# Expert outputs added to the result in device memory by indirect accumulating transfers, in place of a gather and an add per token

## The chip, the cores and the metric

One Trainium2 chip, one core. A time is the device time of one execution in microseconds (us). TensorE (PE) multiplies matrices, VectorE (DVE) and ScalarE (ACT) work on rows, GpSimd (POOL) does the same more slowly and issues the indirect transfers, SyncE (SP) issues most of the plain transfers. Each engine runs its own instructions in order; a transfer is carried out by 16 DMA engines once an engine has issued it.

## The reference, cut to what matters

Everything is fp32. `x` holds 32 x 64 = 2048 tokens of 512 features.

```python
x = x + xattn0(layernorm(x), ctx)          # 32 query heads, 8 key heads, head size 128
x = x + ffn0(layernorm(x))                 # shared MLP 512 -> 1024 -> 512 and a latent path
x = x + xattn1(layernorm(x), ctx)          # 32 heads of size 16
x = x + ffn1(layernorm(x))                 # the part that is changed

def ffn1(h, W_gate, b_gate, W_e, b_e):     # 8 experts, 512 -> 512
    logits = h @ W_gate + b_gate
    _, top_idx = top_k(logits, 2)                             # two experts for each token
    y_all = relu(einsum('bsd,edh->bseh', h, W_e) + b_e)
    return take_along_axis(y_all, top_idx[..., None], 2).mean(axis=2)
```

## The kernel before, in words

The tokens lie in SBUF as 16 tiles `xs[0..15]` of 128 tokens x 512 features, in four chunks of 512 tokens. The kernel goes through the four layers one after the other.

**First attention (0 to about 1240 us).** A loop of 32 steps, each some 38 us long: one group of query heads for one chunk. Two steps that follow each other (a "visit") share a set of weights. `load_attn0` brings the set of the next visit to one of two halves of `weights`. POOL then forms sums of weight quarters: `left_sums` (L396 to L399) of the query weights and `right_sums` (L406 to L409) of the output weights. SP has little else to do in this stage, so that a transfer that waits for nothing is issued long before the step in whose code it stands.

**Lists of the experts.** For the last layer each expert has a list in device memory, `xg`. There are two groups of tokens: chunks 0 to 2 (group 0) and chunk 3 (group 1), and `xg[i]` has room for every token of the group in each of the 8 lists. The lists are set to zero by `clear_lists` (L283), 16 large transfers issued early by SP. Later `route_step` normalizes the rows of a chunk (`norm_row`), multiplies by the gate and finds each token's two experts and its place in their lists (`route_keep`, `route_places`). `route_row` (L1092) then scatters 128 rows at a time to the lists with an indirect transfer from POOL, two for each tile. This runs in the loop of the second attention, in which POOL also computes masks (L926) and the normalized head outputs (`attn1_mix`, L994 to L998). A scatter waits for the clearing transfers of its group.

**Blocks.** A list is worked off in blocks of 128 rows. How many blocks an expert needs is known only at run time, so the program has as many as can be needed: 31 for group 0 and 15 for group 1. `close_lists` computes for each block which expert it belongs to and at which row it starts (`bi`). `load_rows` (L1187, SP) loads four blocks at a time into a tile `xr` after all scatters of the group have landed. `block_turn` transposes a block (4 PE matmuls `px`, an ACT copy to `xT`), and `block_expert` multiplies it by the expert's weights (8 matmuls `py` at L105), adds the bias (DVE, L1217), applies the ReLU with factor 0.5 (ACT, L1218) and stores the 128 rows of `y` to `yg` (ACT, L1219). The tile `y` comes from a pool of seven buffers that `xT` shares, `xr` from a pool of four.

**The end.** When group 0's blocks are done, `gather` (L1223, POOL) fetches the two rows of `yg` that belong to each token of a tile by the places that `token_rows` worked out, and `combine` (L1232, L1233, DVE) adds them to `x` and stores the tile to `out` (L1234, SP). Group 0's tiles are gathered while PE works on group 1's blocks; group 1's four tiles follow after the last block.

Of the kernel before, what the change touches and what calls it, by code (L numbers as in the profile page):

```python
# [9 lines left out]
F32 = mybir.dt.float32  # L10
# [6 lines left out]
P = 128  # L17
# [6 lines left out]
NG = 8  # L24
NE = 8
EPS = 1e-5


@with_exitstack
def layers(ctx: ExitStack, tc: tile.TileContext, a: dict, out: bass.AP):  # L30
# [36 lines left out]

    mix_slots = [cells[:, 10240 + 512 * i : 10752 + 512 * i] for i in range(4)]
    route_rows, route_T = arena[:, 7], arena[:, 6]

    def t8(name):
        return work.tile([P, 4, 512], F32, tag="t8", name=name, bufs=4)

# [189 lines left out]


    GROUPS = [range(0, NC - 1), range(NC - 1, NC)]
    CAP = [len(cs) * CH for cs in GROUPS]
    NB = [2 * cap // P + NE - 1 for cap in CAP]
    xg = [dram.tile([NE * cap, HID], F32, name=f"xg{i}") for i, cap in enumerate(CAP)]
    yg = [dram.tile([nb * P, HID], F32, name=f"yg{i}") for i, nb in enumerate(NB)]

    start_row = const.tile([P, 2, NE], F32, tag="start_row", name="start_row")
    for i, cap in enumerate(CAP):
# [3 lines left out]
        )  # L276
    zero = const.tile([P, P], F32, tag="zero", name="zero")
    nc.gpsimd.memset(zero, 0.0)
# [349 lines left out]
    for i in range(len(order) + 1):  # L628
# [397 lines left out]

    counts, slots = {}, {}

# [32 lines left out]
    def route_places(c, keep):  # L1061
# [19 lines left out]
        pin(nc.vector.tensor_tensor(pos, tot[:, 0], run[:, 0:TT, :], ALU.add))  # L1081
        slots[c] = (pos, keep)
        return chosen(pos, keep, start_row[:, i, :], n)
# [34 lines left out]
    def close_lists(i):  # L1118
# [33 lines left out]
        )  # L1152
        pin(nc.vector.tensor_reduce(blk[:, 0, :], own, AX.X, ALU.add))
        pin(nc.vector.tensor_scalar(blk[:, 0, :], blk[:, 0, :], float(NE - 1), None, ALU.min))
        pin(
# [3 lines left out]
        )  # L1159
        pin(nc.vector.tensor_reduce(blk[:, 1, :], own, AX.X, ALU.add))  # L1160
        pin(nc.vector.tensor_tensor(blk[:, 1, :], steps[0:1, 0:nb], blk[:, 1, :], ALU.subtract))
        pin(
            nc.vector.tensor_scalar(
                blk[:, 1, :], blk[:, 1, :], float(top - 1), float(P), ALU.min, ALU.mult
            )
# [4 lines left out]
        pin(nc.vector.tensor_copy(bi, blk[:, 0:2, :]))  # L1170
        return bi, lst

    def token_rows(i, lst):
        n = f"l{i}"
        off = small.tile([P, NE], F32, tag="off", name=f"off_{n}", bufs=1)
        pin(nc.vector.tensor_scalar(off, lst[:, 1, :], float(P), None, ALU.mult))
        return [chosen(*slots[c], off, f"{n}_{c}") for c in GROUPS[i]]

    def load_rows(i, j0, bi):
        xr = t8(f"xr_{i}_{j0}")  # L1180
        for j in range(j0, min(j0 + 4, NB[i])):
            v = nc.values_load(
                bi[0:1, 1, j : j + 1], engines=[mybir.EngineType.SP],
                min_val=0, max_val=NE * CAP[i] - P,
                skip_runtime_bounds_check_because="an expert's list and a block within it",
            )
# [14 lines left out]

    def block_expert(i, j, xT, bi):
        n = f"{i}_{j}"
# [13 lines left out]
        pin(nc.vector.tensor_tensor(y, py, be1[:, bass.ds(v[1], 1), :], ALU.add))  # L1217
        nc.scalar.activation(y, y, AF.Relu, scale=0.5)  # L1218
        nc.scalar.dma_start(yg[i][j * P : (j + 1) * P, :], y)  # L1219

    def gather(i, u, t, at, ys):
        for r in range(2):
            nc.gpsimd.indirect_dma_start(  # L1223
                out=ys[:, r, :],
                out_offset=None,
                in_=yg[i],
                in_offset=bass.IndirectOffsetOnAxis(ap=at[u][:, r, t : t + 1], axis=0),
            )

    def combine(c, t, ys):  # L1230
        x = xs[c * TT + t]
        pin(nc.vector.tensor_tensor(ys[:, 0, :], ys[:, 0, :], ys[:, 1, :], ALU.add))  # L1232
        pin(nc.vector.tensor_tensor(x, x, ys[:, 0, :], ALU.add))  # L1233
        nc.sync.dma_start(out[(c * TT + t) * P : (c * TT + t + 1) * P, :], x)  # L1234

# [18 lines left out]
    def route_step(c, step):  # L1254
        n = f"e{c}"
        if step in ("rows0", "rows2"):
            t0 = int(step[-1])
            if t0 == 0:
                prep["h"] = route_rows if c < NC - 2 else t8(f"h_{n}")
            stats = row_stats([xs[c * TT + t0 + i] for i in range(2)], f"{n}_{t0}")  # L1260
            for i in range(2):
                norm_row(c, t0 + i, stats, prep["h"][:, t0 + i, :], i)
        elif step in ("turn0", "turn2"):
# [53 lines left out]
    for i in range(NI + 1):  # L1317
# [45 lines left out]
        if c == NC - 1 and b == 6:  # L1363
            lists.append([*close_lists(0)])
        for _ in range(2):
            if sends:
                route_row(*sends.pop(0))
        if c == NC - 1 and b == 1:
            load_experts(range(5, NE))

    blocks = [(0, j) for j in range(NB[0])] + [(1, j) for j in range(NB[1])]
    assert not sends
    first, xr, turned, done, waiting = NB[0], {}, None, 0, []
    between = {
# [3 lines left out]
    for m in range(len(blocks) + 1):  # L1380
        xT = turned
        if m < len(blocks):
            i, j = blocks[m]
            if j % 4 == 0:
                xr[i] = load_rows(i, j, lists[i][0])
            turned = block_turn(i, j, xr[i])
            if m == 0:
                attn1_out(NC * TT - 1, oTs.pop(NC * TT - 1), (0, 1))
        if m > 0:
            il, jl = blocks[m - 1]  # L1390
            block_expert(il, jl, xT, lists[il][0])
        for step in between.get(m, ()):
            route_step(NC - 1, step)
        if sends:
            route_row(*sends.pop(0))
        if m == 13:
            lists.append([*close_lists(1)])
# [69 lines left out]
```

## Time and profile before

| | |
|---|---|
| runs | 2019.36, 2020.13, 2022.64 us; median 2020.13 us |
| profiled execution | 2020.86 us, of which 2019.2 us are its span |
| PE busy | 1939.5 us (96% of the span) |
| DVE, ACT, POOL busy | 50%, 24%, 23% |
| granted clock of TensorE, mean | 0.988 |
| bytes moved by DMA | 155.39 MB |
| time of the first block's `py` / end of the last block's | about 1815 us / 1996.3 us |

A page of the profile gives the busy time of each engine, the chain of work that ended last, and the groups of instructions with the mean duration of one. A transfer's time "to landing" runs from the start of its issue to the semaphore update that says it has landed. Times on the page are microseconds unless they are marked ns.

### The profile page before, as it was taken

To read this page: it belongs to the slowest core of one execution; us is meant where nothing else is said; L and a number is where in the kernel's file an instruction comes from. 1 tells how busy PE (TensorE), PEld (TensorE's weight loads), DVE (VectorE), ACT (ScalarE), POOL (GpSimd) and SP (SyncE) were. 2 spreads that over 40 slices of the span, in tenths; PEclk is the share of its full clock that TensorE was granted. 3 is DMA by queue.
4 is the path that set the end of the run, shared out by engine and by line. 5 is a ranking of instruction groups with operands and counts; after the bars stand their busy time and mean duration, and the time that the engine had idled before them with its cause. 6 is when DMAs were issued, how large, how long until landed. Compare 5 with 4: busy or idle time off the path is not lost.

```text
span 2019.2 us, 26458 instructions
## 1 busy us (share of the span) xinstructions
PE 1939.5 (96%) x10576; PEld 1537.1 (76%) x10576; DVE 1011.8 (50%) x1961; ACT 494.5 (24%) x935; POOL 474.4 (23%) x502
## 2 busy tenths in 40 slices
PE   6999999999999999999999999999999999869995
PEld 5888888888888888888888887778787767545442
DVE  8445445445456445345345355365546676652324
ACT  1211211211212211111111112221113656433221
POOL 5010010010032110110111120144136545541024
PEclk9999999999999999999999999999999999889998
DMA  9993110110120110110110013000014002225457
GB/s 319 284 294 106 35 53 18 35 53 20 54 74 8 45 37 17 52 39 15 52 42 13 21 58 105 1 11 1 1 46 163 17 22 69 84 84 177 155 165 233
DMA packets 138233, 155.39 MB, mean 77 GB/s; under 512 B 5120, under 2 KB 88896, under 8 KB 138112
## 3 DMA queue, kind: packets, MB, share of 16 engines
q1 hardware_dynamic: 126096, 124.53, 19.8%
q0 software_dynamic: 5392, 17.11, 2.6%
q10 hardware_dynamic: 6624, 12.06, 1.6%
q8 instruction: 85, 1.39, 0.3%
q14 instruction: 36, 0.29, 0.0%
HBM read 94.44 MB, written 58.20 MB: 76 GB/s over the span
## 4 chain that ended last, share of the span: by engine, by line
PE 91%; DVE 5%; ACT 1%; DMA 1%; POOL 1%; issue 1%; POOLq 0%; SPq 0%; DVEq 0%; ACTq 0%
PE ppx_o L424 11%; PE pqx_a L424 8%; PE py L105 8%; PE sc_a L105 6%; PE pv_a L105 5%; PE ppz_o L424 5%; PE pqz_a L424 5%; PE pk_a L105 5%; PE po_o L105 3%; PE pp L105 3%; PE pdx_f L424 3%; PE ppy_o L424 3%; PE pqy_a L424 3%; PE pqv_a L424 3%; PE phx_f L424 2%; PE pq_b L105 2%
## 5 line engine op out<-in xcount | busy, mean ns | idle before, releaser
L105 PE MATMUL py<-arena,xT 128*128 x368 | 165.7, 593 | 0.0
L406 POOL TENSOR_TENSOR arena<-weights 128x512 f32<-128x512 f32 x16 | 20.7, 1295 | 563.2 <-PE ppz_o L424 563.2
L365 ACT ACTIVATE at_a<-at_a 128x512 f32<-128x512 f32 x64 | 40.4, 631 | 444.0 <-DVE at_a L364 444.0
L105 PEld LDWEIGHTS pv_a<-weights,arena 128*128 128x128 f32 x1024 | 119.4, 192 | 15.3 <-issue 15.3
L424 PE MATMUL ppx_o<-weights,oT_o 128*128 128x256 f32 x512 | 122.8, 383 | 0.1
L424 PE MATMUL pqz_a<-arena 128*128 128x256 f32 x512 | 121.0, 379 | 1.8 <-DVE qT_a L500 1.8
L105 PE MATMUL pk_a<-arena,weights 128*128 128x512 f32 x256 | 117.7, 603 | 3.6 <-issue 3.6
L424 PE MATMUL pqx_a<-arena,weights 128*128 128x256 f32 x512 | 121.0, 379 | 0.0
L105 PEld LDWEIGHTS sc_a<-kT_a,qT_a 128*128 128x128 f32 x1024 | 119.4, 192 | 1.7
L493 ACT ACTIVATE u_a<-pqx_a,bq 128x256 f32<-128x256 f32 x192 | 80.5, 470 | 163.2 <-PE pqx_a L424 163.2
L105 PE MATMUL pv_a<-weights,arena 128*128 128x128 f32 x1024 | 119.5, 275 | 0.0
L105 PE MATMUL sc_a<-kT_a,qT_a 128*128 128x64 f32 x1024 | 117.9, 273 | 0.0
L105 PEld LDWEIGHTS py<-arena,xT 128*128 128x128 f32 x368 | 66.3, 190 | 65.5 <-issue 65.5
L478 DVE COPY v_a<-pv_a 128x512 f32<-128x512 f32 x32 | 22.1, 690 | 179.8 <-PE pv_a L105 179.8
L584 DVE TENSOR_TENSOR x<-ppx_o,x 128x512 f32<-128x512 f32 x128 | 86.8, 678 | 45.7 <-PE ppx_o L424 43.9
L424 PEld LDWEIGHTS pqz_a<-arena 128*128 128x128 f32 x512 | 97.2, 190 | 15.3 <-issue 2.2
L424 PEld LDWEIGHTS ppx_o<-weights,oT_o 128*128 128x128 f32 x512 | 94.8, 190 | 12.0 <-ACT oT_o L574 0.5
L424 PEld LDWEIGHTS pqx_a<-arena,weights 128*128 128x128 f32 x512 | 94.8, 190 | 11.6
L500 DVE TENSOR_TENSOR qT_a<-pqz_a,u_a 128x512 f32<-128x512 f32 x64 | 44.2, 691 | 112.3 <-ACT u_a L493 80.3
L1217 DVE TENSOR_TENSOR y<-py,weights 128x512 f32<-128x512 f32 x46 | 31.8, 691 | 119.7 <-PE py L105 119.3
L105 PEld LDWEIGHTS pk_a<-arena,weights 128*128 128x128 f32 x256 | 49.3, 194 | 52.9 <-issue 51.5
L396 POOL TENSOR_TENSOR arena<-weights 128x512 f32<-128x512 f32 x18 | 23.2, 1290 | 243.5 <-PE pqz_a L424 240.5
(337 smaller groups left out, 3823.2 us busy)
## 6 DMA issues: line engine op xcount, KB each, us to landing
xg<-zero SPq DMA_DIRECT2D x8, 3072.0 KB, 18.0
weights<-in_Wq SPq DMA_DIRECT2D x16, 1024.0 KB, 5.3
weights<-in_Wo SPq DMA_DIRECT2D x16, 1024.0 KB, 5.2
xr<-xg SPq DMA_DIRECT2D x46, 256.0 KB, 3.4
yg<-y ACTq DMA_DIRECT2D x46, 256.0 KB, 3.0
weights<-in_Wkv SPq DMA_DIRECT2D x32, 256.0 KB, 2.8
arena<-in_ctxT SPq DMA_DIRECT2D x8, 1024.0 KB, 5.1
xg<-zero SPq DMA_DIRECT2D x8, 1024.0 KB, 13.0
```

Source lines behind the costliest of these rows:

```text
L105: nc.tensor.matmul(ps, lhsT, rhs, start=(i == 0), stop=(i == len(pairs) - 1))
L365: nc.scalar.activation(dst, dst, AF.Exp, scale=scale)
L396: engine.tensor_tensor(s1, a21, a22, ALU.add)
L406: engine.tensor_tensor(t1, b12, b11, ALU.subtract)
L424: nc.tensor.matmul(ps[:, m, :], left[:, k, m * P : (m + 1) * P], right[:, k, :], start=first and m == i == k == 0, stop=i == len(pairs) - ...
L478: nc.vector.tensor_copy(v, pv)
L493: nc.scalar.activation(u[:, m * 256 : (m + 1) * 256], ps[:, m * 256 : (m + 1) * 256], AF.Identity, bias=bq[:, 4 * g + 2 * heads + m : 4 * ...
L500: nc.vector.tensor_tensor(q5[:, heads, :, 4 * half : 4 * half + 4, :], ps.rearrange("p (m b q) -> p m b q", m=2, q=64), u.rearrange("p (m ...
L584: nc.vector.tensor_tensor(dst, ps.rearrange("p (m n) -> p m n", m=2), dst, ALU.add)
L1217: pin(nc.vector.tensor_tensor(y, py, be1[:, bass.ds(v[1], 1), :], ALU.add))
```

## The change

A row of a list is now `ROW` = 516 numbers: the 512 features, the token's number as an integer, the factor 0.5, and two numbers that fill it up. `route_step` writes the number and the factor beside the normalized rows with a POOL iota and a POOL memset for each two tiles. An empty row holds zeros, factor 0 and the number of a token of the other group; `clear_list` writes such rows to the lists from a tile `empty` with 130 transfers of 128 rows (97 for group 0, 33 for group 1), and between the groups POOL rewrites `empty`. A list has 128 more such rows at its end, to which the blocks that no expert needs now point.

The residual `x` of each tile is stored to `out` as soon as the second attention is done with it (`attn1_out`). A block's `y` is scaled by its rows' factors in the ReLU, and an indirect transfer from POOL adds its rows to the rows of `out` that the numbers name. `yg`, `token_rows`, `gather` and `combine` are gone. In the built program each such adding transfer waits for the one before it to have landed, for `y` (ACT) and for the load of its `xr`; the first one waits for the stores of `x` as well. Experts 4 to 7 are loaded late where before it was 5 to 7, because the slots beside them have moved by 16 numbers.

```diff
+ROW = HID + 4
-    mix_slots = [cells[:, 10240 + 512 * i : 10752 + 512 * i] for i in range(4)]
-    route_rows, route_T = arena[:, 7], arena[:, 6]
+    mix_slots = [cells[:, 10224 + 512 * i : 10736 + 512 * i] for i in range(4)]
+    route_T = cells[:, 12272:14320].rearrange("p (k n) -> p k n", k=KT)
+    route_rows = cells[:, 14320:16384].rearrange("p (t n) -> p t n", n=ROW)
...
-    xg = [dram.tile([NE * cap, HID], F32, name=f"xg{i}") for i, cap in enumerate(CAP)]
-    yg = [dram.tile([nb * P, HID], F32, name=f"yg{i}") for i, nb in enumerate(NB)]
+    xg = [dram.tile([NE * cap + P, ROW], F32, name=f"xg{i}") for i, cap in enumerate(CAP)]
...
+    def empty_rows(i):
+        nc.gpsimd.memset(empty, 0.0)
+        at = HID - 3 * QUARTER
+        nc.gpsimd.iota(
+            empty[:, at : at + 1].bitcast(I32), pattern=[[0, 1]], base=GROUPS[1 - i][0] * CH,
+            channel_multiplier=1,
+        )
...
-    def clear_lists(e):
-        for i, cap in enumerate(CAP):
+    def clear_list(i, e):
+        if e == 0:
+            empty_rows(i)
+        rows_of = xg[i][e * CAP[i] :, :]
+        for m in range(CAP[i] // P + (e == NE - 1)):
             ins = nc.sync.dma_start(
-                xg[i][e * cap : (e + 1) * cap, :].rearrange("(p m) (k n) -> p (m k) n", p=P, n=P),
-                zero[:, None, :].broadcast_to([P, cap // P * KT, P]),
+                rows_of[m * P : (m + 1) * P, :].rearrange("p (k n) -> p k n", n=QUARTER),
+                empty[:, None, :].broadcast_to([P, 4, QUARTER]),
             )
...
-            if i % 4 == 1:
-                clear_lists(i // 4)
+        if 8 <= i < 24:
+            clear_list(i // 16, i % 8)
...
+            if i == 1:
+                nc.sync.dma_start(out[k * P : (k + 1) * P, :], xs[k])
...
-        nc.scalar.activation(y, y, AF.Relu, scale=0.5)
-        nc.scalar.dma_start(yg[i][j * P : (j + 1) * P, :], y)
-
-    def gather(i, u, t, at, ys):
-        for r in range(2):
+        nc.scalar.activation(y, y, AF.Relu, scale=xr[:, j % 4, HID + 1 : HID + 2])
+        pin(
             nc.gpsimd.indirect_dma_start(
-                out=ys[:, r, :],
-                out_offset=None,
-                in_=yg[i],
-                in_offset=bass.IndirectOffsetOnAxis(ap=at[u][:, r, t : t + 1], axis=0),
-            )
-
-    def combine(c, t, ys):
-        x = xs[c * TT + t]
-        pin(nc.vector.tensor_tensor(ys[:, 0, :], ys[:, 0, :], ys[:, 1, :], ALU.add))
-        pin(nc.vector.tensor_tensor(x, x, ys[:, 0, :], ALU.add))
-        nc.sync.dma_start(out[(c * TT + t) * P : (c * TT + t + 1) * P, :], x)
+                out=out,
+                out_offset=bass.IndirectOffsetOnAxis(
+                    ap=xr[:, j % 4, HID : HID + 1].bitcast(I32), axis=0
+                ),
+                in_=y,
+                in_offset=None,
+                compute_op=ALU.add,
+            )
+        )
...
+            h = prep["h"][:, t0 : t0 + 2, :]
+            nc.gpsimd.iota(
+                h[:, :, HID : HID + 1].bitcast(I32), pattern=[[P, 2], [0, 1]],
+                base=(c * TT + t0) * P, channel_multiplier=1,
+            )
+            nc.gpsimd.memset(h[:, :, HID + 1 :], 0.5)
...
-    load_experts(range(5))
+    load_experts(range(4))
...
-        elif m == 15:
-            rows_of = [token_rows(i, lists[i][1]) for i in range(2)]
-        if m > first + 2 and done < len(GROUPS[0]) * TT:
-            u, t = divmod(done, TT)
-            ys = t4(f"ys_{u}_{t}")
-            gather(0, u, t, rows_of[0], ys)
-            waiting.append((GROUPS[0][u], t, ys))
-            done += 1
-        while waiting and (len(waiting) > 2 or m == len(blocks)):
-            combine(*waiting.pop(0))
-    ys = [t8(f"ys_{t}") for t in range(2)]
-    for t in range(TT):
-        gather(1, 0, t, rows_of[1], ys[t // 2][:, 2 * (t % 2) : 2 * (t % 2) + 2, :])
-    for t in range(TT):
-        combine(NC - 1, t, ys[t // 2][:, 2 * (t % 2) : 2 * (t % 2) + 2, :])
```

More of the change, by code (lines that the diff above doesn't have):

```diff
@@ L65, in layers, with list_rows @@
     ]
-    mix_slots = [cells[:, 10240 + 512 * i : 10752 + 512 * i] for i in range(4)]
-    route_rows, route_T = arena[:, 7], arena[:, 6]
+    mix_slots = [cells[:, 10224 + 512 * i : 10736 + 512 * i] for i in range(4)]
+    route_T = cells[:, 12272:14320].rearrange("p (k n) -> p k n", k=KT)
+    route_rows = cells[:, 14320:16384].rearrange("p (t n) -> p t n", n=ROW)
+    def list_rows(name):
+        return work.tile([P, 4, ROW], F32, tag="t8", name=name, bufs=4)
     def t8(name):
-        return work.tile([P, 4, 512], F32, tag="t8", name=name, bufs=4)
+        t = list_rows(name).rearrange("p i n -> p (i n)")
+        return t[:, 0:2048].rearrange("p (i n) -> p i n", i=4)
     def t4(name):
@@ L276, in layers @@
         )
-    zero = const.tile([P, P], F32, tag="zero", name="zero")
-    nc.gpsimd.memset(zero, 0.0)
+    QUARTER = ROW // 4
+    empty = const.tile([P, QUARTER], F32, tag="empty", name="empty")
+    def empty_rows(i):
[5 more added lines that the diff above has]
+        )
     clearings = ([], [])
     waits = mybir.DependencyInfo(mybir.DependencyClass.Sync, mybir.DependencyReason.DATA)
-    def clear_lists(e):
-        for i, cap in enumerate(CAP):
+    def clear_list(i, e):
[3 more added lines that the diff above has]
+        for m in range(CAP[i] // P + (e == NE - 1)):
             ins = nc.sync.dma_start(
-                xg[i][e * cap : (e + 1) * cap, :].rearrange("(p m) (k n) -> p (m k) n", p=P, n=P),
-                zero[:, None, :].broadcast_to([P, cap // P * KT, P]),
+                rows_of[m * P : (m + 1) * P, :].rearrange("p (k n) -> p k n", n=QUARTER),
+                empty[:, None, :].broadcast_to([P, 4, QUARTER]),
             )
@@ L1024, in attn1_queries @@
             )
-    counts, slots = {}, {}
+    counts = {}
     def route_parts(c, fT):
@@ L1081, in route_places @@
         pin(nc.vector.tensor_tensor(pos, tot[:, 0], run[:, 0:TT, :], ALU.add))
-        slots[c] = (pos, keep)
         return chosen(pos, keep, start_row[:, i, :], n)
@@ L1152, in close_lists @@
         )
-        pin(nc.vector.tensor_reduce(blk[:, 0, :], own, AX.X, ALU.add))
-        pin(nc.vector.tensor_scalar(blk[:, 0, :], blk[:, 0, :], float(NE - 1), None, ALU.min))
+        pin(nc.vector.tensor_reduce(blk[:, 0, :], own[:, :, 0 : NE - 1], AX.X, ALU.add))
         pin(
@@ L1159, in close_lists @@
         )
-        pin(nc.vector.tensor_reduce(blk[:, 1, :], own, AX.X, ALU.add))
+        pin(nc.vector.tensor_reduce(blk[:, 1, :], own[:, :, 0 : NE - 1], AX.X, ALU.add))
         pin(nc.vector.tensor_tensor(blk[:, 1, :], steps[0:1, 0:nb], blk[:, 1, :], ALU.subtract))
@@ L1163, in close_lists @@
             nc.vector.tensor_scalar(
-                blk[:, 1, :], blk[:, 1, :], float(top - 1), float(P), ALU.min, ALU.mult
+                blk[:, 1, :], blk[:, 1, :], float(top), float(P), ALU.min, ALU.mult
             )
@@ L1170, in close_lists @@
         pin(nc.vector.tensor_copy(bi, blk[:, 0:2, :]))
[L1171 to L1177, printed above, removed]
+        return bi
     def load_rows(i, j0, bi):
-        xr = t8(f"xr_{i}_{j0}")
+        xr = list_rows(f"xr_{i}_{j0}")
         for j in range(j0, min(j0 + 4, NB[i])):
@@ L1183, in load_rows @@
                 bi[0:1, 1, j : j + 1], engines=[mybir.EngineType.SP],
-                min_val=0, max_val=NE * CAP[i] - P,
+                min_val=0, max_val=NE * CAP[i],
                 skip_runtime_bounds_check_because="an expert's list and a block within it",
@@ L1200, in block_turn, with block_expert @@
         return xT
-    def block_expert(i, j, xT, bi):
+    def block_expert(i, j, xT, bi, xr):
         n = f"{i}_{j}"
@@ L1258, in route_step @@
             if t0 == 0:
-                prep["h"] = route_rows if c < NC - 2 else t8(f"h_{n}")
+                prep["h"] = route_rows if c < NC - 2 else list_rows(f"h_{n}")
+            h = prep["h"][:, t0 : t0 + 2, :]
[4 more added lines that the diff above has]
+            nc.gpsimd.memset(h[:, :, HID + 1 :], 0.5)
             stats = row_stats([xs[c * TT + t0 + i] for i in range(2)], f"{n}_{t0}")
             for i in range(2):
-                norm_row(c, t0 + i, stats, prep["h"][:, t0 + i, :], i)
+                norm_row(c, t0 + i, stats, prep["h"][:, t0 + i, 0:HID], i)
         elif step in ("turn0", "turn2"):
@@ L1363, in layers @@
         if c == NC - 1 and b == 6:
-            lists.append([*close_lists(0)])
+            lists.append(close_lists(0))
         for _ in range(2):
@@ L1368, in layers @@
         if c == NC - 1 and b == 1:
-            load_experts(range(5, NE))
+            load_experts(range(4, NE))
     blocks = [(0, j) for j in range(NB[0])] + [(1, j) for j in range(NB[1])]
     assert not sends
-    first, xr, turned, done, waiting = NB[0], {}, None, 0, []
+    xr, turned = {}, None
     between = {
@@ L1384, in layers @@
             if j % 4 == 0:
-                xr[i] = load_rows(i, j, lists[i][0])
-            turned = block_turn(i, j, xr[i])
+                xr[i, j // 4] = load_rows(i, j, lists[i])
+            turned = block_turn(i, j, xr[i, j // 4])
             if m == 0:
@@ L1390, in layers @@
             il, jl = blocks[m - 1]
-            block_expert(il, jl, xT, lists[il][0])
+            block_expert(il, jl, xT, lists[il], xr[il, jl // 4])
         for step in between.get(m, ()):
@@ L1396, in layers @@
         if m == 13:
[L1397 to L1412 removed]
+            lists.append(close_lists(1))
 def kernel(
```

## The prediction

> **What bounds the kernel now.** I read the page first, then the chain of work that ended last, then the end of the span by stretches and in order of time, then the rows of the transfers.
>
> ```profile
> span 2019.2 us, 26458 instructions
> PE 1939.5 (96%) x10576; PEld 1537.1 (76%) x10576; DVE 1011.8 (50%) x1961; ACT 494.5 (24%) x935; POOL 474.4 (23%) x502
> ```
>
> PE is busy nearly throughout, so time is to be had only where PE idles. The chain (start, length, what) ends so:
>
> ```profile
> 1981.63 3.44 PE py L105 x8
> 1985.50 3.43 PE py L105 x8
> 1989.37 6.88 PE py L105 x16
> 2009.75 4.86 DMA ys<-yg,at_l
> ```
>
> PE sets the pace to 1996.3, one block each 3.87 us (1985.50 to 1989.37). What follows is not PE's. The stretches (length, busy time of PE, PEld, DVE, ACT, POOL with counts, clock, DMA share, GB/s):
>
> ```profile
> 1900.00:1950.00 50.00, 50.00 (x155) 24.54 (x154) 8.95 (x13) 14.48 (x26) 5.43 (x6) 1.00 0.44 141
> 1996.50:2019.20 22.70, 0.00 (x0) 0.00 (x0) 8.59 (x13) 0.63 (x1) 8.03 (x8) 0.59 0.59 182
> ```
>
> For the last 22.7 us PE does nothing. The instructions there (start, length, engine, idle before it and releaser):
>
> ```profile
> 2000.55 0.95 POOL L1223 DMA_INDIRECT ys<-yg,at_l  x1 [7.03 <-DMA yg<-y]
> ...
> 2009.75 0.95 POOL L1223 DMA_INDIRECT ys<-yg,at_l  x1 [0.31 <-issue]
> ...
> 2014.70 0.69 DVE L1232 TENSOR_TENSOR ys<-ys 128x512 f32<-128x512 f32 x1 [0.50 <-DMA ys<-yg,at_l]
> 2015.43 0.69 DVE L1233 TENSOR_TENSOR x<-x,ys 128x512 f32<-128x512 f32 x1
> ```
>
> The last `y` is stored, eight gathers are issued one after the other, the last lands, two adds follow, and the store's landing ends the span. This is what the change can win. The rows of indirect transfers, issue and time to landing (min, median, max), first the scatters from 1724 to 1800 us, then the last eight gathers:
>
> ```profile
> L1092 POOL DMA_INDIRECT xg<-h_e,at_e x7: 979/1000/1007, 1774.8 to 1795.2; - x7
> ...
> DMA to landing us min/median/max: 2.7/2.8/4.4
> ```
> ```profile
> L1223 POOL DMA_INDIRECT ys<-yg,at_l x8: 947/953/1334, 2000.5 to 2009.8; - x8
> ...
> DMA to landing us min/median/max: 3.4/4.1/5.5
> ```
>
> **The change part by part.** All sums are made against the span of 2019.2 us. The profiled execution took 2020.86 us, 1.66 more than its span and 0.73 over the median of 2020.13; I carry the difference over to the median.
>
> *The end, if the adding transfers keep up.* PE's work is the same, so the last `py` still ends at 1996.3. DVE's bias (0.69) and ACT's ReLU (0.63) bring `y` at 1997.7; one adding transfer of time T then ends the span. With T = 3.8 that is 2001.5: 17.7 less. Gone with it are 32 gathers (0.95 each on POOL), 32 DVE adds (0.69 each) and 46 stores on ACT; PE's cover hides all but those of the last 22.7 us, so they count for nothing more.
>
> *The chain of adding transfers.* The program has 46, and each is issued only when the one before it has landed: nothing overlaps between them. The first can go when the first `y` is there (1820.4, from ACT's rows) and the last tile of `x`, finished by PE's `pp` at 1814.8, is stored (landing 3.1 us): about 1821.5. If T is over 3.87 us, PE is slowed after a few blocks, since `xT` takes over the buffer of the `y` five blocks back, and `xr` that of rows whose adds have landed; from then on the end is 1821.5 + 46 T. That meets 2019.2 at T = 197.7 / 46 = 4.30 us. So T decides the sign.
>
> The trace has no adding transfer. Its nearest row is the scatter: 2.8 us, of which 1.0 is POOL's issue. After a landing the next issue takes some 0.2 us more (the scatter of 1803.0 lands after 2.8, and SP issues the load that waited for it at 1806.04). By that row alone T = 3.0, and all 46 hide under PE. Against it stands the Trainium skill, "Collectives: The Full Stack", section "The bandwidth ceiling: the fold count and why AG ≠ RS ≠ AR": an add in the transfer itself costs no extra cycles, but two reads through the same ring, so the moving part takes twice as long. From the row of the indirect queue (5392 packets, 2.6% of 16 engines) the 64 indirect transfers hold the engines for 0.026 x 2019 / 64 = 0.82 us each; by the rule another 0.82. The second read is from device memory, as a gather's is, and a gather lands at best after 3.4 us where a scatter's median is 2.8: 0.6 more. The sum is 2.8 + 0.8 + 0.6 + 0.2 = 4.4. A load of `xr` (1 MB for four blocks) shares the DMA engines in every four blocks, and eight scatters of group 1 go between the adds, 1.27 us apart in the trace and with landings up to 5.6 there: I add 0.1 and take T = 4.5. Low end 3.0, high end 5.7 (the longest landing of a gather). With 4.5 the end is 1821.5 + 207 = 2028.5, 9.3 later than now. By the row alone it would be 17.7 earlier.
>
> *POOL's queue at the end.* Behind an add that waits stand only the eight scatters of group 1, one after each of the blocks 8 to 15. Group 1's loads come at block 31, so some 15 blocks cover them. Nothing else of the kernel waits for POOL there.
>
> *The empty rows at the start.* Before, 16 zero transfers; now 130 of 264 KB, 34.3 MB against 33.6. Both begin at 28 us. SP issues them at about 0.7 us each (as its loads from 25.05 to 27.09 go) and they need more in the engines: the trace moves zeros in 512-byte pieces at
>
> ```profile
> 100.00:140.00 40.00, 40.00 (x220) 34.26 (x219) 19.21 (x32) 7.43 (x16) 5.03 (x4) 1.00 1.01 288
> ```
>
> 288 GB/s, that is 0.92 us each. The new wait: POOL rewrites `empty` only when all 97 transfers of group 0 have read it, and in POOL's order this memset stands just ahead of the third visit's `left_sums`. They start now at 141.0 (L396), and PE needs their second sum at
>
> ```profile
> 175.08 1.92 PE pqx_a L424 x8
> ```
>
> and the second sum takes POOL 2.5, so POOL can be held to about 172. Up to the memset 27.1 MB have to move from some 33 us on (97 transfers and 1.5 MB of weights): 94 us at the trace's rate, done at 127. The pieces are now 516 bytes and mostly start off a 256-byte boundary. No row shows such pieces; the Trainium skill, "DMA: Bandwidth & Descriptors", section "How a descriptor splits into AXI transactions", counts 16 beats for 512 aligned bytes and, by its rule, about 20 for 516 at an average offset. With that ratio, 1.25, it is done at 150, so POOL is late but PE is not: cost 0, covered by 22 us. At twice the time (221) PE would stand still for 49 us; bounds 0 and +49. SP's queue: the third visit's output weights now stand behind all 97, and so arrive at about 160, needed at 190.9 (L406); the fourth visit's stand behind the 33 others, 36 to 45 us later, and are needed at 216.6 at the earliest. Both are covered.
>
> *The second attention.* Eight iotas (0.14 us each, as L273) and eight memsets (0.15, as L219) on POOL make 2.3 us; PE waits for POOL only 4.0 us from 1760 to 1800, and the ones for group 0 stand earlier, so they are hidden by PE's other work. The iota for chunk 1 also waits for chunk 0's scatters, as DVE does today (3.9 us in all), with the head outputs queued behind it: up to 3. I take +1 for both. The 16 stores of `x` (0.33 us each on SP, landing 3.1) stand ahead of the first load of `xr`, save the last; their data are there by 1801.6, that load goes at 1806.0, so 4 us cover them: 0. The one more late expert (6.1 us to landing) is not needed before its first block, some ten blocks in: 0. ACT's ReLU takes its factor from a column; ACT is a quarter busy: 0. DVE loses 26 small operations off the path: 0.
>
> *Sum:* +9.3 (chain of adds in place of the end) + 0 (start) + 1 (second attention) = +10.3, so 2020.13 + 10.3 = 2030.4.
>
> **The rivals.**
> - *The adds keep up* (faster). For it: the scatter's 2.8 us and the 0.9 us between it and a block's time. Against it: the second read. T = 4.1 gives 1821.5 + 188.6 = 2010.1, 9 less; T of 3.87 or below gives the floor, 2020.1 - 17.7 + 1 = 2003. It decides below T = 4.2.
> - *My forecast:* the serial chain takes PE's place, T from 4.4 to 5.7, 2024 to 2085.
> - *The start stalls* (slower): the 516-byte pieces are so slow that POOL's memset, and behind it the `left_sums`, come after 172. It decides by itself if the empty rows of group 0 take over 1.5 times today's time for a byte; at 1.6 it costs 33 + 150 - 172 = 11 us, at 2 49 us, and alone with adds that keep up it would give 2003 + 11 to 49.
> - *T over 5.7:* reading and writing a row may not overlap; at T = 7 the end is 2143.
>
> That the adds are not serial can be left out: the waits are in the program.
>
> **How the numbers follow.** What the measurement can tell from no change is about 0.2%, 4 us, that is T from 4.19 to 4.37 with the rest at +1. Chances: serial chain with T to 5.7 0.50; adds keep up 0.31; within 4 us 0.05; a stall at the start that decides 0.09; T over 5.7 0.05. Faster 0.31, same 0.05, slower 0.64. The time is that of the likeliest, 2030. The range takes the floor with some 5 us for the +1 and the last landing below, 1998, and T = 5.7 above, 2085; the likeliest case alone spans 2024 to 2085.
>
> **What would show it.** Right: the adds from POOL stand at equal distances of about 4.5 us, each released by the landing of the one before; PE idles between blocks from about the sixth on, waiting for ACT's `xT`, which waits for an add; DVE and PE are idle at the end for one T only. The distance between two adds is the number to read first. POOL's memset of `empty` at about 150 with no PE wait after it shows the start right. Wrong: adds spaced 3.87 with PE full to 1996 (the first rival), a PE wait for POOL's `left_sums` near 175 (the third), or PE's last stretch before 1815 moved by more than 3 us, which no step here foresees.

## The result, and the profile after

| | before | after |
|---|---|---|
| median (runs) | 2019.74 us (4) | 2139.91 us (4), 2135.19 to 2144.52 |
| ratio | | 1.059, 95% interval 1.057 to 1.062 |
| profiled span | 2019.2 us | 2138.7 us |

The change makes the kernel 5.9% slower. The forecast was slower, but by 10 us, not by 120, and the time lies above the forecast range of 1998 to 2085 us. The first lines of the page after:

```profile
span 2138.7 us, 26535 instructions
PE 1955.0 (91%) x10576; PEld 1540.6 (72%) x10576; DVE 987.0 (46%) x1901; ACT 498.7 (23%) x935; POOL 517.1 (24%) x535
```

PE has the same 10576 matmuls, but its share falls from 96% to 91%. Two new waits say where (engine, what, line, what it waited for: us in total, times, longest), in the list of waits of the kernel after:

```profile
PE py L111 <- DVE y L1231: 54.6, 30, 3.6
PE pqx_a L443 <- POOL arena L416: 41.3, 1, 41.3
```

The second is a single stall near the start. These stretches of the kernel after show it (columns as in the prediction's stretches, GB/s last):

```profile
100.00:140.00 40.00, 40.00 (x220) 34.26 (x219) 19.22 (x31) 7.44 (x15) 5.03 (x4) 1.00 1.12 169
150.00:180.00 30.00, 25.30 (x151) 21.21 (x150) 14.58 (x24) 5.24 (x9) 0.00 (x0) 0.98 1.15 150
180.00:210.00 30.00, 0.00 (x0) 0.00 (x0) 0.00 (x0) 0.00 (x0) 0.00 (x0) 0.50 1.16 148
```

From 180 to 210 us no engine computes; the DMA engines are busy throughout (share 1.16) and yet move 148 GB/s, where the kernel before moved 288 at 100 to 140 us. What ended it, in POOL's instructions in order of time:

```profile
213.58 0.21 POOL L289 MEMSET empty<- 128x129 f32 x1 [87.99 <-DMA xg<-empty]
...
215.30 1.26 POOL L416 TENSOR_TENSOR arena<-arena,weights 128x512 f32<-128x512 f32 x1
```

POOL waited 88 us for the transfers of group 0 to have read `empty`; PE's second sum (L416) stands right behind the memset.

The first wait is the chain of adds. The rows of `out` in the kernel after (duration of an issue in ns, min/median/max, then first and last start in us):

```profile
L1234 POOL DMA_INDIRECT out<-y,xr x46: 1534/1542/1684, 1862.6 to 2129.7; - x46
...
  DVE y L1231: 173.2, 33
```

(2129.7 - 1862.6) / 45 = 5.94 us from add to add, where a block of PE takes 3.87. The second line stands under "who waited for it": the bias of DVE waited 173 us for buffers that an add still held. The distances are not all alike. POOL's adds where four blocks are loaded into `xr` (SP issues these loads from 1956.98 us on):

```profile
1952.01 1.55 POOL L1234 DMA_INDIRECT out<-y,xr  x1 [2.68 <-issue]
...
1957.45 1.56 POOL L1234 DMA_INDIRECT out<-y,xr  x1 [2.59 <-issue]
1965.05 1.55 POOL L1234 DMA_INDIRECT out<-y,xr  x1 [6.04 <-DMA out<-y,xr]
```

The distance beside the loads is 7.60 us, the one before it 5.44, though a scatter stands in that one. It is so all along the chain: the eight distances in which such loads fall are 6.8 to 7.7 us, the others 5.5 in the median, with a scatter between the adds or without. Near the end no load runs beside the adds; POOL's instructions there:

```profile
2102.87 1.54 POOL L1234 DMA_INDIRECT out<-y,xr  x1 [3.82 <-issue]
...
2124.38 1.54 POOL L1234 DMA_INDIRECT out<-y,xr  x1 [3.83 <-issue]
2129.74 1.54 POOL L1234 DMA_INDIRECT out<-y,xr  x1 [3.82 <-DMA out<-y,xr]
```

(2129.74 - 2102.87) / 5 = 5.37 us each: 1.54 of issue and 3.83 idle. The chain of the kernel after splits the last one another way:

```profile
2124.38 4.61 DMA out<-y,xr
2128.99 0.03 POOLq L1234
2129.02 0.50 issue
```

The add has landed 4.61 us after its start, and the next starts 0.75 us after that. The profile puts most of POOL's idle time in this chain down to "issue" (148.0 us of it) and only 3 waits to the landing before; that the landing is what they wait for is shown further down.

**The sum of the difference.** The spans differ by 119.5 us. The first add starts at 1862.6, where 1821.5 was forecast: 41.1, in the main the stall at the start. From the first add to the end it is 2138.7 - 1862.6 = 276.1, where the kernel before has 2019.2 - 1821.5 = 197.7 from the same forecast point: 78.4, the chain and what follows it. Together 119.5. The experiments took the two apart; all but the two full versions at the end were run once, each beside the kernel before, whose own times in these experiments lie between 2019 and 2026 us.

### The profile page after: what moved, and what is told of

Same layout as the page of the kernel before. It is cut to its first block, busy times and chain, and to the rows that moved or that the text cites. A ratio compares the mean times of both kernels' runs of the same rounds, so it can differ in the third digit from the quotient of the medians.

```text
span 2138.7 us, 26535 instructions
## 1 busy us (share of the span) xinstructions
PE 1955.0 (91%) x10576; PEld 1540.6 (72%) x10576; DVE 987.0 (46%) x1901; ACT 498.7 (23%) x935; POOL 517.1 (24%) x535
## 5 line engine op out<-in xcount | busy, mean ns | idle before, releaser
L111 PE MATMUL py<-arena,xT 128*128 x368 | 176.1, 622 | 58.4 <-DVE y L1231 54.6
L425 POOL TENSOR_TENSOR arena<-weights 128x512 f32<-128x512 f32 x16 | 20.7, 1293 | 532.9 <-PE ppz_o L443 532.9
L1234 POOL DMA_INDIRECT out<-y,xr x46 | 71.3, 1550 | 199.9 <-issue 148.0
L111 PE MATMUL pv_a<-weights,arena 128*128 128x128 f32 x1024 | 119.5, 275 | 0.0
L443 PE MATMUL pqx_a<-arena 128*128 128x256 f32 x256 | 65.1, 398 | 41.3 <-POOL arena L416 41.3
```

The costliest lines, as they stand in the source:

```text
L111: nc.tensor.matmul(ps, lhsT, rhs, start=(i == 0), stop=(i == len(pairs) - 1))
L425: engine.tensor_tensor(t1, b12, b11, ALU.subtract)
L443: nc.tensor.matmul(ps[:, m, :], left[:, k, m * P : (m + 1) * P], right[:, k, :], start=first and m == i == k == 0, stop=i == len(pairs) - ...
L1234: nc.gpsimd.indirect_dma_start(out=out, out_offset=bass.IndirectOffsetOnAxis(ap=xr[:, j % 4, HID : HID + 1].bitcast(I32), axis=0), in_=y, ...
```

## Experiments on the start

Theory: the 516-byte pieces of the empty rows go at half the speed, because most of them start off some boundary. Rivals: it is POOL's wait for `empty` that costs, whatever the speed; or it is the number or the length of the pieces.

**Two tiles of empty rows (s1_two_tiles).** The kernel after, with POOL's wait gone.

```diff
-    empty = const.tile([P, QUARTER], F32, tag="empty", name="empty")
+    empties = [cells[:, 15872 + 256 * i : 15872 + 256 * i + QUARTER] for i in range(2)]
```

> The changed kernel, with one tile of empty rows for each group, so that POOL does not wait to rewrite one. Theory (the pieces of 516 bytes are slow, and POOL's wait is only the first that shows it): the stall of 41.3 us at pqx of the third visit goes, but the 130 transfers still end near 270 us, the fourth visit's query weights stand behind most of them on SP and land near 268, and PE, which needs their second sum at 250.7, now waits some 15 to 25 us there: about 2140 - 41 + 20 = 2119 us. Rival (POOL's wait is the whole of it): all 41 us come back, 2099 us.

Measured 2150.18 us (the kernel before beside it 2025.6): no gain, and 31 us over what the theory expected. PE's waits in this run:

```profile
PE pqx_a L444 <- DMA weights<-in_Wq: 25.4, 1, 25.4
PE ppx_o L444 <- DMA weights<-in_Wo: 22.9, 1, 22.9
```

With POOL free, the weights of the next visits are late instead, 48.3 us in two stalls where 15 to 25 were expected: they stand behind the empty rows in SP's queue. POOL's wait was only the first place where slow pieces hurt; this rival is out.

**Whole rows (s2_whole_rows).** Each empty row in one piece of 2064 bytes; two small tables lie in the tile `empty` later, to make room.

```diff
-    empty = const.tile([P, QUARTER], F32, tag="empty", name="empty")
+    empty = const.tile([P, ROW], F32, tag="empty", name="empty")
...
-                rows_of[m * P : (m + 1) * P, :].rearrange("p (k n) -> p k n", n=QUARTER),
-                empty[:, None, :].broadcast_to([P, 4, QUARTER]),
+                rows_of[m * P : (m + 1) * P, :],
+                empty,
```

> The changed kernel, with empty rows written as one piece of 2064 bytes each instead of four of 516; still one tile that POOL rewrites after group 0's transfers (the small tables of the block list are laid into that tile later, for room). Theory (the cost is in the pieces: each of 516 bytes takes about as long as two of 512): 264 KB move at 250 GB/s or more, group 0's 97 transfers are done by about 140 us, no stall: 2140 - 41 = 2099 us. Rival (the number of transfers, 130 in place of 16, or SP's issue at 0.7 us and more each): the rate stays near 150 to 170 GB/s and the stall near 41 us: 2140 us.

Measured 2096.83 us, span 2095.1: 43.6 less than the kernel after. The stretch and the adds of this run:

```profile
100.00:140.00 40.00, 40.00 (x219) 34.26 (x220) 19.22 (x31) 7.51 (x14) 5.63 (x6) 1.00 0.92 319
```
```profile
L1234 POOL DMA_INDIRECT out<-y,xr x46: 1534/1542/1683, 1823.2 to 2086.4; - x46
```

319 GB/s, no stall of PE at the start, and the first add 1.7 us from the 1821.5 of the forecast. So the pieces were the whole of the first part, and neither the 130 transfers nor SP's issue of them was, since both stayed; what remains over the kernel before, 2095.1 - 2019.2 = 75.9 us of span, lies in the adds and what follows them. Whether it was the length or the starts (here at multiples of 16 bytes) is not told by this run.

**The kernel before with its zeros shifted.** Four runs leave the 512-byte pieces of the kernel before as they are, or make them a row long, and move only where they start (the first numbers of the lists are not cleared): by one number (s3, shown here), four (s4), sixteen (s5), and by one with `n=HID` and a tile `zero` of that width (s6, where two small tables lie in `zero` later). The lists have one row more, for room.

```diff
-                xg[i][e * cap : (e + 1) * cap, :].rearrange("(p m) (k n) -> p (m k) n", p=P, n=P),
+                xg[i].rearrange("r n -> (r n)")[e * cap * HID + 1 : (e + 1) * cap * HID + 1].rearrange(
+                    "(p m n) -> p m n", p=P, n=P
+                ),
```

> The kernel before, its 16 zero transfers written 4 bytes further on in device memory, in the same pieces of 512 bytes (the first four bytes of the lists are not cleared). Theory (what makes a piece slow is that it does not begin and end on a boundary in device memory): the rate from 100 to 140 us falls from 288 to some 150 to 180 GB/s, the transfers end near 240 us instead of 166, weights of the third and fourth visits come late behind them: 2020 + 10 to 40 us. Rival (the 516 bytes' length, or the number of transfers): 288 GB/s and 2020 us as before.

> As s3, but shifted by 16 bytes instead of 4 (the first 16 bytes of the lists are not cleared). Rows of 2064 bytes in s2 begin at multiples of 16 and were fast. Theory A (a start off a multiple of 16 bytes is what is slow): 288 GB/s from 100 to 140 us and 2020 to 2026 us. Theory B (any start off a boundary of 64 bytes or more is slow for short pieces, and in s2 the length of a piece hides it): some 140 to 200 GB/s, PE waiting for weights, 2050 to 2106 us.

> The kernel before with its zero pieces of 512 bytes all starting 64 bytes off (the rows' last 64 bytes are left as they are; the lists' clearing is so not the same). If what is slow is a start off a 64-byte boundary: 100 to 140 us moves at about 288 GB/s as in the kernel before, no PE wait for weights, and about 2022. If it is a start off a boundary of 256 bytes or of the piece's own length[...]: about 150 GB/s and a PE wait of some 44 us as with 16 bytes, about 2075[...].

> The kernel before with its zeros in pieces of 2048 bytes (a whole row) in place of 512, all starting 4 bytes off. If a long piece hides the bad start (two ends for 2048 bytes in place of eight): over 250 GB/s at 100 to 140 us, no PE wait, about 2022. If it was the starts at multiples of 16 bytes that made the whole rows fast: about 140 GB/s as in the run of 512-byte pieces shifted by 4, and 2075 to 2106.

The stretch from 100 to 140 us of the four, in this order: 4 bytes off, 16 bytes off, 64 bytes off, and 4 bytes off with pieces of 2048 bytes:

```profile
100.00:140.00 40.00, 40.00 (x220) 34.26 (x219) 19.21 (x31) 7.42 (x15) 5.03 (x4) 1.00 1.18 139
```
```profile
100.00:140.00 40.00, 40.00 (x220) 34.26 (x219) 19.23 (x32) 7.52 (x15) 5.04 (x4) 1.00 1.22 151
```
```profile
100.00:140.00 40.00, 40.00 (x220) 34.26 (x219) 19.21 (x31) 7.42 (x15) 5.02 (x4) 1.00 1.18 267
```
```profile
100.00:140.00 40.00, 40.00 (x219) 34.26 (x220) 19.18 (x31) 7.57 (x14) 5.03 (x4) 1.00 1.08 258
```

| | GB/s | us | kernel before beside it |
|---|---|---|---|
| 512 bytes, 4 off | 139 | 2106.38 | 2025.6 |
| 512 bytes, 16 off | 151 | 2075.56 | 2022.65 |
| 512 bytes, 64 off | 267 | 2016.13 | 2022.4 |
| 2048 bytes, 4 off | 258 | 2021.86 | 2022.4 |

By a shift of 4 bytes alone, with the same number, length and order of transfers, the kernel before slows its zeros at least as much as the change did and loses 81 us, twice what was expected. In the first two of the four PE then waits for weights, as in the run with two tiles; in the first:

```profile
PE ppx_o L426 <- DMA weights<-in_Wo: 69.7, 1, 69.7
```

A shift of 64 bytes costs little in speed and nothing in time. So the boundary lies above 16 and at or under 64 bytes (32 was not tried). A shift moves the end of a piece with its start, and which of the two counts was not tried. And a long piece hides most of the bad start: 258 GB/s at the same 4 bytes. A fixed price for each piece fits this only in part: by these rates, which are of all 16 engines together, 512 bytes take 1.78 ns at 288 GB/s and 3.68 at 139, 1.9 more; 2048 bytes with the same 1.9 added to 7.11 would go at 227, and went at 258. What sets the price stays open. Length and start are told apart all the same: the whole rows start at multiples of 16 bytes, where 512-byte pieces went at 151 GB/s, and so won by being long.

## Experiments on the adds

Theory: each add waits for the landing of the one before, and the addition in the transfer makes that landing long. Rivals: the DMA engines or POOL's issue can do no more than one add in 5.4 us; or it is the indirect addressing, not the addition.

**Plain writes (c1_plain, c4_plain_whole_rows).** The adds become plain indirect writes, first in the kernel after and then in the one with whole rows.

```diff
-                compute_op=ALU.add,
```

> The changed kernel with the 46 adding transfers as plain indirect writes to out, which leaves out the addition; every wait between them stays. Theory (the addition in the transfer makes it long: POOL's issue 1.54 against 1.00 us, the transfer 2.2 against 0.8): one write every 3.6 us and some 4.1 when rows are loaded beside it, against 5.94; PE with 3.87 a block is the bound or nearly: 1862.6 + 46 x 3.9 to 4.2, about 2045 to 2057 us. Rival (the chain of waits itself costs, whatever is transferred): distance over 5 us, 2100 us or more.

Measured 2079.4 us, where 2045 to 2057 was expected. The writes stand (2068.9 - 1886.9) / 45 = 4.04 us apart, as expected, but the start stalled for 62.8 us in this run, longer than in the kernel after (41.3), with 150 and then 133 GB/s from 100 to 180 us; why this was slower than in the kernel after is not known. So its total mixes two things, and the run with whole rows is the cleaner one.

> The kernel with empty rows written whole (as in s2), and the adding transfers as plain indirect writes, which leaves out the addition. Nothing else differs from s2. Theory (the two costs add up, and the addition is what makes the chain slow): the chain begins near 1823 as in s2 and then takes the 190.8 us that it took in c1, so the span ends near 2014, 2016 us in all, below the kernel before by 4 to 10 us; the addition's price is 2097 - 2016 = 81 us. Rival (c1 was fast because PE came late and lists lay ready): 2040 us or more.

Measured 2013.6 us (before 2022.65), span 2011.9:

```profile
L1234 POOL DMA_INDIRECT out<-y,xr x46: 969/969/1025, 1822.9 to 2003.1; - x46
```

180.2 / 45 = 4.0 us from write to write, against (2086.4 - 1823.2) / 45 = 5.85 with the addition. Without the addition and without the slow pieces the change would win 9 us, by one run of each. So the indirect addressing alone would have cost nothing here. The addition by itself costs 2096.83 - 2013.6 = 83 us. With these the difference of the spans splits a second time: 43.6 (pieces) + 83.2 (addition) - 7.3 (all the rest) = 119.5.

The chain of this run has landings of 2.76 us where the adds have 4.61:

```profile
1999.56 2.76 DMA out<-y,xr
2002.32 0.03 POOLq L1234
2002.35 0.51 issue
```

The next write starts at 2003.09, again 0.77 us after the landing. This part is the same in both chains; the other 1.85 belong to the addition. 0.57 of them are POOL's issue (1.54 against 0.97). The rest fits what the packets take. The row of the indirect queue (packets, MB, share of 16 engines), with whole rows and adds, then with whole rows and plain writes; the scatters in it are the same:

```profile
q0 software_dynamic: 9456, 20.84, 5.4%
```
```profile
q0 software_dynamic: 6512, 20.84, 2.7%
```

(0.054 x 2095.1 - 0.027 x 2011.9) / 46 = 1.28 us more in the 16 engines for each transfer.

**Two targets (c2_two_targets).** Whole rows, and the adds go by turns to `out` and to a second tensor, so that an add waits only for the one before the last; `x` is stored to both, and the two are not summed.

```diff
-                out=out,
+                out=targets[j % 2],
```

> The s2 kernel whose adds go in turn to out and to a second tensor of the same size, so that each waits for the last but one; x is stored to both, and the sum of the two is left out. Theory (waiting for the one before is what makes the transfers' 5.5 us count): two are in flight, PE with 3.87 us a block is the bound again, the last block's py ends near 1999 and the span near 2005, 2007 us in all, with some us more for the 16 added stores. Rival (the DMA engines or POOL's issue of 1.54 us are the limit, not the wait): distance between adds stays over 5 us and 2060 us or more.

Measured 2005.42 us (before 2022.65). The 24 adds to `out`:

```profile
L1236 POOL DMA_INDIRECT out<-y,xr x24: 1534/1542/1787, 1817.6 to 1994.9; - x24
```

177.3 / 45 = 3.94 us from add to add: PE's own pace is nearly back, and no wait of PE for `y` is left. At this pace neither the DMA engines nor POOL limit the adds; the wait for the landing did. The landing records of the run with whole rows say the same: of the 45 adds after the first, 42 start 0.74 us after the landing of the one before.

**Half the bytes (c3_half).** Whole rows, each add with 256 of the 512 columns, to a tensor half as wide; the other half is left out.

```diff
-                in_=y,
+                in_=y[:, 0 : HID // 2],
```

> The s2 kernel with adds of half the columns to a tensor of half the width (the other half is left out, and out gets only x). The number of rows and all waits stay. Theory (the moving part goes by bytes): 1.4 us of a transfer's packets halve, distance 5.5 to about 4.9 where nothing else moves, 46 x 0.6 less: about 2070 us. Rival (the cost is by row: reading a row, adding and writing it back have a fixed part): distance within 0.2 of 5.5, about 2095 us.

Measured 2049.3 us (before 2022.65):

```profile
L1236 POOL DMA_INDIRECT half_out<-y,xr x46: 1534/1542/1650, 1822.3 to 2039.6; - x46
```

217.3 / 45 = 4.83 us, 1.02 less than with all columns, and the issue is the same 1.54. By doubling this, an estimate, about 2 us of an add go by its bytes, more than expected. In the trace's packet records an add's packet carries one row of 2048 bytes in 178 ns in the median, but 247 in the mean, since some, mostly the first of an add, take several times as long; half a row takes 102 and 137. The plain write's packet carries two rows, 4096 bytes, in 169 ns by both.

## Versions built from this

**Two sums, merged (v1_two_sums).** What two targets win is kept and the sum is made whole: for each group two sums in device memory, one begun with `x`, one with zeros; they are fetched, added on DVE and stored to `out`, twelve tiles beside the blocks of group 1 and four at the end.

```diff
-                out=out,
+                out=sums[i][j % 2],
...
+    def fetch(c, t, ys):
+        i, at = c // (NC - 1), slice((c * TT + t) * P, (c * TT + t + 1) * P)
+        for r in range(2):
+            nc.sync.dma_start(ys[:, r, :], sums[i][r][at, :])
+
+    def finish(c, t, ys):
+        pin(nc.vector.tensor_tensor(ys[:, 0, :], ys[:, 0, :], ys[:, 1, :], ALU.add))
+        nc.sync.dma_start(out[(c * TT + t) * P : (c * TT + t + 1) * P, :], ys[:, 0, :])
```

> A version built from what the runs showed: whole-row empty rows, and the adds of a group go by turns to two sums in device memory (one begun with x, one with zeros), so that an add waits only for the one before the last; the two sums are fetched, added on DVE and stored as the output: twelve tiles of group 0 beside the blocks of group 1, four tiles after the last block. Theory (the wait of one add for the landing of the one before is what costs; loads and one DVE add are cheap where they lie beside blocks): adds about 3.9 us apart, no PE wait for the buffer of y; PE's last py ends at about 1996, the last add lands about 2001, two loads 3.5, an add 0.7, a store 3.1: span about 2009, so about 2011, 10 us under the kernel before, ratio 0.995. Rival (the twelve merged tiles, 768 KB of loads and stores beside the adds, lengthen each landing beyond 7.7 us or hold SP's queue): adds over 4.2 us apart in group 1 and 2020 or more, no gain.

Measured 2027.71 us, ratio 1.0027 (1.0018 to 1.0036): no gain, a little slower. From 1881.6 to 1982.2 us the adds stood 3.87 us apart on the mean, until the merge caught up with its own loads; the last four distances are 4.9 to 5.5. DVE's instructions then:

```profile
1985.31 0.69 DVE L1260 TENSOR_TENSOR ys<-ys 128x512 f32<-128x512 f32 x1 [4.33 <-DMA ys<-sum]
1985.92 0.69 DVE L1240 TENSOR_TENSOR y<-py,weights 128x512 f32<-128x512 f32 x1
```

DVE waits 4.33 us for a merge's load with the bias of the next `y` (L1240) queued behind it. SP had issued that load late, since the load waits for an earlier tile's store to land (nine such waits of SP, 36.3 us in all), and the following store stands behind it in SP's queue.

**The merge moved aside (v2_two_sums).** The stores of the merged tiles go on ACT's queue, DVE adds one block earlier, and the four last tiles are all fetched before the first is added.

```diff
-        nc.sync.dma_start(out[(c * TT + t) * P : (c * TT + t + 1) * P, :], ys[:, 0, :])
+        queue.dma_start(out[k * P : (k + 1) * P, :], own)
...
+            finish(k, ys[:, 0, :], ys[:, 1, :], nc.scalar)
```

> The version with two sums again, with its merge of group 0 out of the way of y: the merged tiles' stores go on ACT's queue in place of SP's (where a load of two tiles later stood waiting ahead of each store, some 5.9 us for a tile), the loads begin as before and the adds of DVE one block earlier each; at the end the four tiles' sums are all fetched before the first add, those of the parity that is done first, and the four stores go on two queues. Theory (what held the first version back was DVE waiting 3 to 5 us for those loads ahead of y's bias in each of the last eight blocks, and SP's queue at the end): adds stay 3.87 us apart to the last, issued at about 1998 and landed at 2003; fetch 4.5, add 0.7, stores 4: span 2012 to 2014, so about 2014, 0.4% under the kernel before. Rival (the loads and stores lengthen each add's landing beyond 7.7 us wherever they are put): adds over 4.2 us apart in the last ten blocks and 2022 or more.

Measured 2017.11 us against 2021.04, ratio 0.9979 (0.9971 to 0.9988): the one full version that beats both kernels, the kernel before by 0.2%. The adds to the sums, first v1, then v2:

```profile
L1243 POOL DMA_INDIRECT sum<-y,xr x46: 1534/1542/1783, 1819.7 to 2003.2; - x46
```
```profile
L1243 POOL DMA_INDIRECT sum<-y,xr x46: 1535/1542/1916, 1822.0 to 1999.3; - x46
```

The last add goes 3.9 us earlier, and what follows it takes 2014.8 - 1999.3 = 15.5 us in place of 20.4. Of the 22.7 us that followed PE's work before, 17.2 are still there (from DVE's last bias at 1997.58 to 2014.8), most of them the merge of the last four tiles. The time came out 3 us above what was expected.

## Why the prediction was wrong, point by point

- **The direction and the mechanism of the chain were right.** The adds are serial, PE waits from then on, and the end is the first add plus 46 T. With T = 5.94 in place of 4.5, 46 T is 273 of the 276 us measured. Two steps failed: the speed of the pieces at the start, and the size of T.
- **The start: the step that failed is the speed of the 516-byte pieces.** The working took the ratio 1.25 from the Trainium skill, "DMA: Bandwidth & Descriptors", section "How a descriptor splits into AXI transactions", and put the memset at 150. It came at 213.6, a ratio of 288/150 = 1.9. The rest of that step held: it said POOL can be late until 172, and 213.6 - 172 = 41.6 is what PE waited (41.3). By the rule's count a start 16 bytes off should cost 17 beats against 16; the run shows 151 GB/s against 288. At 64 bytes off the count is 18, from which 256 GB/s can be estimated, and the run shows 267. The count thus misses the price of a start off the boundary found here.
- **SP's queue: "both are covered" did not hold either** once the pieces were slow. It was hidden behind POOL's wait, and two tiles of empty rows brought it out.
- **T: three terms of the sum were too small.** The addition costs 1.85 us, not 1.4: the rest of it, 1.28, was covered by the 0.8 and 0.6 of the sum, but POOL's longer issue, 0.57, had no term. The next issue comes 0.75 us after a landing, not 0.2, which had been read from SP's queue, not from POOL's. And the loads of `xr` beside the adds make 5.94 - 5.37 = 0.57 on the mean, not 0.1; the scatters make no difference that the trace shows. Together T is 1.44 us longer, 65 us over 45 steps.
- **The rule of two reads fell short of the time here.** In the median the 128 packets of 178 ns are 2.1 times the 64 of 169 ns of the plain write, near the twofold time that the prediction took from the Trainium skill, "Collectives: The Full Stack", section "The bandwidth ceiling: the fold count and why AG ≠ RS ≠ AR". In the mean an add's packets hold the engines for 128 x 247 / 16 = 1.97 us against 64 x 169 / 16 = 0.68, 2.9 times; and from the first to the last packet of an add it is 2.3 us against 0.83.
- **The end had a term that was left out.** The span ends 9.0 us after the last add's start, not 4.5.
- **The second attention (+1)** cannot be judged: in the six runs with whole rows the first add starts anywhere from 1817.6 to 1823.2, around the forecast 1821.5.
- **The range was put together wrongly.** Its upper end, 2085, took the longest T with no stall at the start, and the stall was costed only beside adds that keep up. The two do not exclude each other: the bounds that stood in the text, 49 us and T = 5.7, give 2134 together, still 6 us under the measurement. Both cases that had been given small chances came true, the stall and a T over 5.7, and their sum, 41.1 + 69.1 - 1 = 109.2, is the whole miss in the span (69.1 is 276.1 less the forecast 207, and 1 the second attention's).

## What to carry to other kernels

A chain of transfers that wait for each other is priced by the distance between two of them, not by a landing: add the queue's restart and what runs beside it, and multiply before believing that cover exists. Split a chain over two targets where it is the wait and not the engine that limits, but count the merge, which gave back most of the gain here. When a row gets wider, ask where each piece of a transfer now starts; write the row whole, or keep short pieces on the boundary (64 bytes off was fast here, 16 was not). And costs with different causes add: the upper end of a range must hold them together.

## What was not expected of the hardware

- Writes of zeros to device memory in 512-byte pieces ran at half the speed (139 and 151 GB/s against 288) when they started 4 or 16 bytes off, at 267 when 64 bytes off; in pieces of 2048 bytes, 4 off, at 258.
- An indirect transfer of 128 rows that adds held POOL 1.54 us against 0.97 for a plain write, at both widths tried (512 columns, and 256 in c3_half).
- POOL started the next of a chain of indirect transfers about 0.75 us after the landing it waited for, adding (0.75) or not (0.77).
- The runs whose last transfer is POOL's ended late: the last packet is through at 2134.0 in the kernel after and at 2005.5 with plain writes and whole rows, and the spans end 4.7 and 6.4 us later; before and in v2, with a store of SP as the last, 1.4 and 1.6 us later. Why is not shown.
